# A four-layer graph network on one core: layers 1 to 3 as rounds of small steps in a fixed order

## The chip, the core and the metric

The kernel runs on one core of a Trainium2 chip. The metric is the device time of one execution in microseconds; the time of a kernel is the median of several executions.

The core's engines run beside each other and meet at semaphores. TensorE (PE in the profile; its weight loads are PEld) does matrix products and transposes and writes them to PSUM, eight banks of 128 x 512 fp32 here. VectorE (DVE) and ScalarE (ACT) do elementwise work and read PSUM. GpSimd (POOL) issues the indirect DMAs that gather rows by index. SyncE (SP) and ScalarE's queue issue the other transfers.

## The reference

`x` holds 4096 nodes of 256 features, `adj` is a symmetric 4096 x 4096 matrix of zeros and ones with ones on the diagonal; each entry off the diagonal is set with a chance of about 0.2%, so a node has some nine neighbours. Four graph attention layers follow each other, each on the layer-normed input and added to it:

```python
h = jnp.maximum(_layernorm(x, axis=-1), 0.0); x = x + _L0_gnn_ref(...)   # 8 heads, curvature bias
h = jnp.maximum(_layernorm(x, axis=-1), 0.0); x = x + _L1_gnn_ref(...)
h = jnp.maximum(_layernorm(x, axis=-1), 0.0); x = x + _L2_gnn_ref(...)
h = jnp.maximum(_layernorm(x, axis=-1), 0.0); x = x + _L3_gnn_ref(...)

# layer 1: one head
h = node_features @ W.T + b_W
e = (h @ a1)[:, None] + (h @ a2)[None, :] + b_a[0]
e = jnp.where(e > 0, e, 0.2 * e)
attention = jax.nn.softmax(jnp.where(adjacency_matrix > 0, e, NEG_INF), axis=1)
h_prime = attention @ h

# layer 2: e of both signs (e the leaky_relu of Wh1 + Wh2.T), then one product
h_prime = softmax(where(mask, e, NEG_INF)) @ inp
h_prime_negative = -softmax(where(mask, -e, NEG_INF)) @ inp
elu(concatenate([h_prime, h_prime_negative], axis=1) @ wtrans)

# layer 3: four heads of 64
h = x @ w.T + bias
score = leaky_relu(h @ h.T, 0.01)
coeff = softmax(where(adj > 0, score, 1.0)); relu(coeff @ h)
```

## The kernel before

**Lists instead of the matrix.** Layer 0 finds each node's neighbours in `adj` and keeps them as lists; layers 1 to 3 use the lists only. Nodes lie in NT = 32 tiles of P = 128. For each tile the edges are sorted into EC = 9 chunks of 128, one edge on each partition. An *indirect DMA* fetches for every edge of a chunk the neighbour's row from a table in DRAM (`table1`, `table2`, `table3`, one for each layer, written tile by tile during the layer before): `gather`, L909, on GpSimd, one instruction for each chunk. The rows land in `g`, a buffer of nine chunks and the tile's own rows; there are G = 6 such buffers. `st` is a 0/1 matrix that says which edge belongs to which node of the tile, `s` the same with edges on the other side; `sw` is `s` weighted with the edge's softmax weight.

**What a tile needs.** The sum over neighbours, "attend", is a chain of matrix products of `sw` with `g` (`summed`, L930; in layer 2 `attend2`, L1919), and the last column gives the softmax's denominator, whose reciprocal `inv` is taken on VectorE by the step that finishes the tile. In layers 1 and 3 the ninth chunk (LATE) isn't gathered: its rows come from the table's last eighth, held in SBUF as three bf16 parts (`late_rows`), and are picked by a product with a 0/1 matrix `to` (`expanded`, L1701, then a copy to `g` on ScalarE, L1705). So layers 1 and 3 gather 8 chunks for each tile and layer 2 gathers 9.

- Layer 1: `marked` and `go_to` build `st` and `to` from the lists; `before1` spreads the nodes' scores over the edges by products with `st` (`by_edge`) and keeps `s` for layers 2 and 3 in DRAM (`s_of`; `st` and `to` go to `rows_of`); `weigh1` makes scores, exponentials and `sw`; `attend1`; `finish1` divides, adds to `x` and normalizes; `rows2` makes `table2`'s row by VectorE and ScalarE; `give2` makes layer 2's own scores for each edge.
- Layer 2: `weigh2` makes `sw` with both signs (L1897 to L1906); `attend2` two chains, one for each half of the tile's nodes; `signed2` scales both by their reciprocals (L1929 to L1934); `turn_signed` transposes (L1941) and copies to `two_t` (ScalarE, L1945); `through_wt` multiplies by `wtrans` (L1954); `finish2`, `turn3` and `rows3` make `x`, its transpose `hT` and `table3`'s row.
- Layer 3: `before3` casts `s` on ScalarE; `weigh3` spreads the tile's own rows over the edges (27 products into the PSUM buffers `pv`, L2056), multiplies by `g` on VectorE (L2060), sums within heads (L2061), takes the exponential and weights `g` (L2074); `attend3`; `finish3`.

**Order.** Layers 1 to 3 are each one call of `run` (L1714). It takes a list of steps with lags: the step of tile t is issued in round t + lag, and within a round in the order of the list. `loads` (lag -3), `begin` (the first 7 chunks of gathers, lag 2 - G = -4) and `begin_late` (the rest, later for the first tiles, as the end of the table is written last) are ahead of the list. Layer 3's list, for example:

```python
[(0, weigh3), (1, attend3), (-1, before3), (2, finish3), (-1, expand3), (-2, own_parts)]
```

TensorE runs in the order of this program (`manual_schedule`). VectorE, ScalarE, GpSimd and the DMA queues get their order from the scheduler, which sees the dependencies and a few `issue_after` hints; each engine runs its own list strictly in order. Layer 0 is ordered by a planner that the change leaves alone.

Of the kernel before, what the change touches and what calls it, by code (L numbers as in the profile page):

```python
# [9 lines left out]
F32 = mybir.dt.float32  # L10
# [694 lines left out]
BEHIND = 3  # L705
ROW0, ROW1, ROW3 = C + H0 + CF, C + 2, C
# [7 lines left out]
def gnn_lists(  # L714
# [917 lines left out]
    with tc.tile_pool(name="work", bufs=2) as work, tc.tile_pool(name="kept", bufs=1) as kept:  # L1632
# [9 lines left out]
        mine1 = kept.tile([P, MINE, P + 3], BF16, name="mine1")  # L1642
        nc.gpsimd.tensor_copy(mine1[:, :, :P], ident_b[:, None, :].to_broadcast([P, MINE, P]))

        def by_edge(pool, t, st, own_t):

            my = mine1[:, t % MINE, :]
            nc.any.tensor_copy(my[:, P:], upper(own_t))
            s, parts = spread(pool.tile([P, 3, 512], F32, name="s_ps"), st, my, P + 3)
            a = work.tile([P, EC + 1], F32, name="a", bufs=3)  # L1650
            nc.vector.tensor_reduce(a[:, :EC].rearrange("p (b c) -> p b c", c=3), parts, AX.X, OP.add)
            return s, a
# [31 lines left out]
        def go_to(t, to):  # L1684

            pm = bank(ps_e, "pe")[:, :P]
            nc.tensor.matmul(
                pm, lhsT=col_late[:, t : t + 1].to_broadcast([P, P]), rhs=ident, start=True, stop=True
            )
            nc.vector.tensor_tensor(  # L1690
                to.rearrange("p (b e) -> p b e", b=LB), pm[:, None, :].to_broadcast([P, LB, P]),
                late_no[:, :, None].to_broadcast([P, LB, P]), op=OP.is_equal,
            )

        def expanded(t, of, width, pool, name):

            to = of.pop("to")
            ps = bank(pool, name)[:, :width]
            for b in range(LB):
                for i in range(3):  # L1700
                    nc.tensor.matmul(  # L1701
                        ps, lhsT=to[:, b * P : (b + 1) * P], rhs=late_rows[:, b, i, :width],
                        start=(b == 0 and i == 0), stop=(b == LB - 1 and i == 2),
                    )
            nc.scalar.copy(of["g"][:, LATE, :width], ps)  # L1705
# [8 lines left out]
        def run(table, width, x_of, steps, first=None, expand=False, rows=True):  # L1714


            of, late = [{} for _ in range(NT)], {}

            def loads(t):
                two = t // 2 * 2  # L1720
                if t == two:
                    of[t]["ss"] = work.tile([P, 2, EC * P], BF16, name="ss", bufs=3)
                    if not first:
                        nc.sync.dma_start(of[t]["ss"], s_of[t // 2])
                of[t]["pair"] = of[two]["ss"]
                of[t]["s"] = by_slot(of[t]["pair"][:, t - two, :])
                if rows:
                    if t == two:
                        of[t]["sts"] = work.tile([P, 2, (EC + LB) * P], BF16, name="st", bufs=4)
                        if not first:  # L1730
                            nc.sync.dma_start(of[t]["sts"], rows_of[t // 2])
                    both = of[two]["sts"][:, t - two, :]
                    of[t]["st"], of[t]["to"] = both[:, : EC * P], both[:, EC * P :]
                if first:
                    marked(first, t, of[t]["st"])
                    go_to(t, of[t]["to"])
                    if t > two:
                        store(rows_of[t // 2], of[two]["sts"])
# [6 lines left out]
            def begin(t):  # L1745
                with ExitStack() as queue:
                    if t - BEHIND in late:
                        queue.enter_context(tc.issue_after(late.pop(t - BEHIND).ins))
                    of[t]["g"] = gather_early(t, table, width, g_pool)

            def begin_late(t):
                last = gather_late(t, of[t]["g"], table, width, range(EARLY, LATE if expand else EC))
                if t < G - BEHIND:
                    late[t] = last

            def late_lag(t):

                return (-1, -2, -2, -3, -3)[t] if t < 5 else 2 - G

            steps = [(-3, loads), (2 - G, begin), (late_lag, begin_late)] + [  # L1760
# [444 lines left out]
```

## Time and profile before

| | |
|---|---|
| median of 11 runs | 2046.18 us (2035.33 to 2054.24) |
| profiled execution, its own time | 2041.4 us |
| its span | 2039.6 us, granted TensorE clock 0.814 |
| layer 0, 1, 2, 3 in its trace | 0 to 735, to 1150, to 1635, to 2039.6 us |
| busy in the span | PE 69%, PEld 53%, DVE 57%, ACT 34%, POOL 54% |
| gathers | 1088 (288, 256, 288, 256), mean 981 ns, 1067.3 us in all |

Times in views are microseconds from the start of the span, and means are in ns. A number in brackets after an instruction is the idle time of its engine before it, with what released it. A matmul's end is modelled, not recorded. "issue" is time in which an engine waited for nothing that the profile shows; "remote" and "another core or an unknown queue" stand for a release whose source the profile does not find.

### The profile page before, as it was taken

The page shows a single profiled execution, that of the slowest core. Times are in us where ns is not written, and L with a number is a line of the kernel's source. Part 1 is how long each engine was busy: PE and PEld are TensorE (multiplying, and loading weights), DVE is VectorE, ACT ScalarE, POOL GpSimd, SP SyncE. Part 2 cuts the span into 40 slices and gives each one's busy share as a digit, 9 for nine tenths or more (in the row PEclk, how much of TensorE's full clock was granted, in tenths as well). Part 3 has the DMA queues.
Part 4 walks back from the last instruction along what each step waited for, and adds up shares of the span by engine and source line. Part 5 has one row for each costly group of instructions (what it writes and reads, how often), then busy time and mean ns, then how long its engine had stood idle before and what let it go on. Part 6 is the DMA issues. An engine that isn't in the chain of part 4 may idle for free.

```text
span 2039.6 us, 24838 instructions
## 1 busy us (share of the span) xinstructions
PE 1398.7 (69%) x7536; PEld 1081.6 (53%) x7536; DVE 1159.6 (57%) x3174; ACT 686.6 (34%) x1798; POOL 1095.3 (54%) x1179
## 2 busy tenths in 40 slices
PE   5735545757576765767578347888889478888886
PEld 3413434535454544556457235666668356666665
DVE  5635645756674544555356224555556258877886
ACT  4545434635442233333233013333334221111111
POOL 2063354445556457667565566666661456656640
PEclk9855767867777867788788669888889689989998
DMA  8866666766434455666567545555553356656630
GB/s 271 290 223 199 196 191 207 237 198 208 130 103 123 131 155 157 199 191 200 158 201 245 169 110 164 157 171 166 164 161 114 110 166 206 208 180 207 194 110 23
DMA packets 169888, 356.67 MB, mean 175 GB/s; under 512 B 32272, under 2 KB 104208, under 8 KB 169744
## 3 DMA queue, kind: packets, MB, share of 16 engines
q0 software_dynamic: 52224, 145.30, 26.9%
q1 hardware_dynamic: 67970, 143.98, 21.5%
q10 hardware_dynamic: 49550, 65.71, 9.1%
q8 instruction: 62, 1.02, 0.2%
q14 instruction: 82, 0.67, 0.1%
HBM read 291.66 MB, written 63.21 MB: 174 GB/s over the span
## 4 chain that ended last, share of the span: by engine, by line
PE 39%; DVE 18%; another core or an unknown queue 18%; issue 11%; ACT 5%; DMA 2%; POOL 1%; ACTq 0%; DVEq 0%; POOLq 0%; SPq 0%
PE o L930 20%; PE o L1919 5%; PE pt L1954 3%; PE pv L2056 2%; PE pt L874 2%; DVE g L2074 2%; PE pv L1701 2%; PE pe L1701 1%; DVE s L2061 1%; DVE v L2060 1%; POOL g L909 1%; DMA g<-table,nbr 1%; DVE sw L1897 1%; DVE g L1537 1%
## 5 line engine op out<-in xcount | busy, mean ns | idle before, releaser
L909 POOL DMA_INDIRECT g<-table,nbr x1088 | 1067.3, 981 | 763.4 <-issue 319.1
L930 PE MATMUL o<-g,sw 128*128 128x257 f32 (+1 forms) x1216 | 320.9, 423 | 6.8 <-remote 3.2
L930 PEld LDWEIGHTS o<-g,sw 128*128 128x128 f32 x1216 | 257.0, 214 | 55.0 <-issue 4.0
L1919 PE MATMUL o<-g,sw 128*128 128x257 f32 x896 | 207.9, 390 | 12.1 <-issue 12.1
L1919 PEld LDWEIGHTS o<-g,sw 128*128 128x128 f32 x896 | 177.7, 198 | 40.8 <-issue 12.2
L930 PE MATMUL o<-g,s_f 128*128 128x264 f32 x576 | 167.8, 456 | 0.0
L930 PEld LDWEIGHTS o<-g,s_f 128*128 128x128 f32 x576 | 136.0, 236 | 33.0
L1954 PE MATMUL pt<-wt_s,two_t 128*128 128x256 f32 x256 | 91.2, 518 | 60.1 <-ACT two_t L1945 57.6
L1204 ACT ACTIVATE mask<-adj,minus_half 128x1024 bf16<-128x1024 int32 x112 | 125.1, 1143 | 19.6 <-PE kps L1226 5.2
L2056 PE MATMUL pv<-parts,st 128*128 128x256 bf16 x864 | 111.4, 278 | 26.4 <-issue 21.9
L865 PE MATMUL pt<-ident,r 128*128 128x128 f32 x192 | 45.2, 324 | 106.4 <-DVE r L845 33.1
L2060 DVE TENSOR_TENSOR v<-pv,g 128x512 f32<-128x512 f32 (+1 forms) x160 | 94.0, 630 | 42.0 <-remote 29.6
L2056 PEld LDWEIGHTS <-st 128*128 128x128 bf16 x864 | 84.7, 100 | 49.5 <-issue 38.8
L1954 PEld LDWEIGHTS pt<-wt_s,two_t 128*128 128x128 f32 x256 | 63.7, 259 | 83.1 <-ACT two_t L1945 67.2
L2065 ACT ACTIVATE pm<-s 128x40 f32<-128x40 f32 x32 | 6.7, 208 | 297.9 <-DVE s L2063 240.5
L1701 PEld LDWEIGHTS <-st 128*128 128x128 bf16 x768 | 74.8, 100 | 49.9 <-issue 35.6
L2074 DVE SCALAR_TENSOR_TENSOR g<-pm,g 128x2560 f32<-128x2560 f32 x32 | 90.3, 2823 | 7.1 <-issue 5.8
L865 PEld LDWEIGHTS pt<-ident,r 128*128 128x128 f32 x192 | 25.8, 161 | 126.8 <-issue 57.1
L1537 DVE TENSOR_TENSOR g<-g,pt 128x2560 f32<-128x2560 f32 x32 | 90.1, 2815 | 1.9 <-ACT pt L1534 1.3
L874 PE MATMUL pt<-wcat,hT 128*128 128x272 f32 (+1 forms) x256 | 75.8, 422 | 15.1 <-issue 9.7
L930 PE MATMUL o<-g,ident 128*128 128x264 f32 (+1 forms) x128 | 57.7, 541 | 39.6 <-DVE g L2074 20.1
L2061 DVE TENSOR_REDUCE s<-v 128x36 f32<-128x2304 f32 x32 | 81.7, 2553 | 1.1
(360 smaller groups left out, 2344.6 us busy)
## 6 DMA issues: line engine op xcount, KB each, us to landing
adj<-in_adj_l SPq DMA_DIRECT2D x128, 512.0 KB
ss<-s_of SPq DMA_DIRECT2D x32, 576.0 KB
g<-table,nbr POOLq DMA_INDIRECT x1088
rows_of<-st ACTq DMA_DIRECT2D x16, 832.0 KB
st<-rows_of SPq DMA_DIRECT2D x16, 832.0 KB
x<-x SPq DMA_DIRECT2D x24, 512.0 KB
s_of<-ss ACTq DMA_DIRECT2D x16, 576.0 KB
table<-row ACTq DMA_DIRECT2D x32, 258.0 KB
```

Source lines behind the costliest of these rows:

```text
L874: nc.tensor.matmul(pp, lhsT=hT[:, k, :], rhs=w[:, k, :], start=(k == 0), stop=(k == KC - 1))
L909: last = nc.gpsimd.indirect_dma_start(out=g[:, c, :width], out_offset=None, in_=table[: NE if c < EARLY else N, :], in_offset=bass.Indirec ...
L930: nc.tensor.matmul(o, lhsT=a, rhs=b, start=(i == 0), stop=(i == len(pairs) - 1))
L1204: nc.scalar.activation(m, a, AF.Sign, bias=minus_half, scale=1.0)
L1537: nc.vector.tensor_mul(gh, gh, w[:, :, :, None].to_broadcast([P, K, H0, D0]))
L1701: nc.tensor.matmul(ps, lhsT=to[:, b * P : (b + 1) * P], rhs=late_rows[:, b, i, :width], start=(b == 0 and i == 0), stop=(b == LB - 1 and i ...
L1919: nc.tensor.matmul(o, lhsT=sw[:, h, i].rearrange("p s r -> p (s r)"), rhs=g[:, c, : C + 1], start=(i == 0), stop=(i == HC + 1),)
L1954: nc.tensor.matmul(pp, lhsT=lhs[:, k, :], rhs=wt_s[:, k, :], start=(k == 0), stop=(k == 2 * KC - 1))
L2056: nc.tensor.matmul(pv[:, k, :], lhsT=st[:, (a + k) * P : (a + k + 1) * P], rhs=parts[:, i, :], start=(i == 0), stop=(i == 2),)
L2060: nc.vector.tensor_mul(v[:, a : a + n, :], pv[:, :n, :], g[:, a : a + n, :C])
L2061: nc.vector.tensor_reduce(s[:, :EC, :], heads(v, K3), AX.X, OP.add)
L2074: weighed3[t] = nc.vector.scalar_tensor_tensor(gh, w[:, :, :, None].to_broadcast([P, K, K3, D3]), -math.e, gh, op0=OP.add, op1=OP.mult,)
```

## The change

The steps of layers 1 to 3 are cut into smaller ones, most of them with work for one engine, and get new lags and a new order. A step that reads what TensorE wrote (`take1`, `go_to`, `take2`, `take_signed`, `take3`, `low2`, `row3`, `multiply3`, the `finish` steps) is now apart from the one that made it, and is issued at another place of the round or a round later. In rounds 0 to 31 of each layer, `in_order` adds an ordering dependency without a semaphore between each two successive instructions of VectorE and of ScalarE, so these two run in the order in which the program issues them.

```diff
+        def in_order(first):
+            traced = nc.cur_bb.bb.instructions
+            for engine in (nc.vector.engine, nc.scalar.engine):
+                mine = [i for i in traced[first:] if i.engine == engine]
+                for a, b in zip(mine, mine[1:]):
+                    tc.add_manual_dep(b, a.name, mybir.DependencyInfo(
+                        mybir.DependencyClass.NoSync, mybir.DependencyReason.DATA), reason="round")
...
-            def late_lag(t):
-                return (-1, -2, -2, -3, -3)[t] if t < 5 else 2 - G
-            steps = [(-3, loads), (2 - G, begin), (late_lag, begin_late)] + [
+            lead = last_use + 1 - G
+            def late_lag(t):
+                return first_use - 1 + t // 2 - t if t < 5 else lead
+            steps = [(-3, loads), (lead, begin), (late_lag, begin_late)] + [
...
             for r in sorted(rounds):
+                if r == 0:
+                    start = len(nc.cur_bb.bb.instructions)
+                if r == NT + 0:
+                    in_order(start)
...
-                    (3, give2), (0, weigh1), (2, finish1), (1, attend1), (-1, before1),
-                    (2, rows2), (-1, expand1),
-                first=only, expand=True,
+                    (-1, take1), (-1, score1), (0, attend1), (-3, go_to), (3, take2), (1, finish1),
+                    (2, store2), (-3, off1), (-1, weigh1), (-2, spread1), (-2, expand1), (-3, mark1), (-4, look_up),
+                    (2, give2), (1, rows2), (-3, keep_rows),
+                last_use=0, first_use=-1, rows=True,
...
-                    (0, weigh2), (1, signed2), (2, finish2), (0, attend2), (2, turn3), (1, turn_signed),
-                    (2, rows3), (1, through_wt),
-                rows=False,
+                    (-1, score2), (0, attend2(0)), (2, through_wt), (-1, weigh2), (1, signed2), (3, turn3),
+                    (3, take3), (0, attend2(1)), (4, row3), (2, low2), (1, turn_signed), (4, parts3), (2, finish2),
+                    (3, rows3), (1, take_signed),
+                last_use=0, first_use=-1, late=2, s=True,
...
-            name="l3_v", bufs=5, space=PSUM
+            name="l3_v", bufs=1, space=PSUM
...
+            def products3(t, of, first, last):
+                for i in range(first, last):      # pv0 to pv4, a bank each
+                    ...
             def expand3(t, of):
-                if t:
-                    expanded(t, of, C, ps_v, "pv")
+                pv = bank(ps_v, f"pv{GV - 1}").rearrange("p (k c) -> p k c", c=C)
+                of.setdefault("pv", {})[GV - 1] = pv
+                expand_to(pv[:, 1, :], of.pop("to"), C)
+            def spread3(t, of):
+                products3(t, of, 0, GV - 1)
+            def take3(t, of):
+                nc.scalar.copy(of["g"][:, LATE, :C], of["pv"][GV - 1][:, 1, :])
+            def last3_of(t, of):
+                products3(t, of, GV - 1, GV)
...
-                [(0, weigh3), (1, attend3), (-1, before3), (2, finish3), (-1, expand3), (-2, own_parts)],
-                expand=True,
+                    (-3, own_parts), (5, out3), (1, total3), (1, full3), (0, multiply3), (2, attend3),
+                    (0, score3), (0, exp3), (3, finish3), (4, add3), (-1, expand3), (-1, spread3),
+                    (-1, take3), (-1, last3_of), (0, weigh3),
+                last_use=2, first_use=0, s=True, rows=True,
```

`lead` makes the early gathers' lag -5 in layers 1 and 2 and -3 in layer 3, where attend moves from lag 1 to lag 2; the number of buffers stays 6. In layer 3 the five PSUM buffers `pv`, used in turn by `expand3` and the products, become `pv0` to `pv4` with one place each, and `expand3` writes the second half of `pv4`, whose first half `last3_of` fills. Some work changes engines: in layers 1 and 2 the copy of one column for each tile goes from ScalarE to VectorE; in layer 3 the self weight (VectorE, L2066) becomes a ScalarE activation, and `finish3`'s product with `inv` (VectorE) becomes four ScalarE activations (Relu with a scale), followed by an addition on VectorE in `add3`. Stores move with their steps: `table2` to `store2` (a round later than `finish1`), `xs[1]` to `rows2`, `out` to `out3`.

## The prediction

> **What bounds the kernel now.** I read the page's chain first, then POOL's groups by layer, the timeline around the longest gap, and a table of stretches. The chain by engine, from the page:
>
> ```profile
> PE 39%; DVE 18%; another core or an unknown queue 18%; issue 11%; ACT 5%; DMA 2%; POOL 1%; ACTq 0%; DVEq 0%; POOLq 0%; SPq 0%
> ```
>
> There is one core, so 18% "another core" (some 360 us when its pieces are added up, about 200 of it in layers 1 to 3) has no such cause. I looked for what those pieces have in common. The longest, as the timeline has it (start, duration, engine, instruction, idle time before and its releaser):
>
> ```profile
> 1176.16 0.60 PE L1941 MATMUL pt<-ident,two 128*128 128x128 f32 x4
> ...
> 1183.43 0.17 DVE L1929 RECIPROCAL inv<-o 128x1 f32<-128x1 f32 x1 [7.52 <-remote]
> 1197.82 0.95 POOL L909 DMA_INDIRECT g<-table,nbr  x1 [0.30 <-issue]
> 1203.05 0.32 SPq L923 DMA_DIRECT2D g<-table  x1
> 1203.06 0.17 DVE L1929 RECIPROCAL inv<-o 128x1 f32<-128x1 f32 x1 [19.14 <-remote]
> 1203.29 0.94 POOL L909 DMA_INDIRECT g<-table,nbr  x1 [4.53 <-remote]
> 1204.65 1.65 PE L1954 MATMUL pt<-wt_s,two_t 128*128 128x256 f32 x3 [27.89 <-ACT two_t L1945]
> ```
>
> TensorE had finished `attend2` by about 1176.3, yet VectorE took the product 7 and 27 us later. In between GpSimd gathered without a break from 1154.3 to 1198.8 (35 gathers); 4 us after its last one everybody who waited for TensorE went on at the same moment. The other long pieces (14.3 us at 770, 17.0 at 967, 15.2 at 1130, 15.7 at 1601) fall in the same way into unbroken runs of 24 to 28 gathers. So in this trace a product of TensorE is seen late while GpSimd gathers on; after a run of 8 or 9 gathers the lag is 2 to 4 us. The reason is not shown; the pattern is.
>
> GpSimd's gathers by layer (layers 1, 2, 3; busy us, mean ns, idle before and what ended it):
>
> ```profile
> L909 POOL DMA_INDIRECT g<-table,nbr x228 | 235.7, 1034 | 114.0 <-issue 62.0 <-PE o L930 21.1 <-remote 9.3
> ```
> ```profile
> L909 POOL DMA_INDIRECT g<-table,nbr x260 | 255.7, 983 | 140.8 <-issue 72.9 <-remote 21.8 <-PE pt L865 19.0
> ```
> ```profile
> L909 POOL DMA_INDIRECT g<-table,nbr x228 | 215.7, 946 | 147.4 <-issue 60.0 <-DMA table<-row 26.2 <-PE pv L2056 21.5
> ```
>
> At 0.30 us between gathers, a tile costs POOL 8 × 1.334 = 10.7, 9 × 1.283 = 11.5 and 8 × 1.246 = 10.0 us. The attends came every 12.0, 13.4 and 11.7 us. The rest of POOL's idle time is waiting for TensorE to free a buffer `g`: 114.0 − 228 × 0.30 = **45.6**; 140.8 − 260 × 0.30 − 12.5 (before the first gather, the table's write) = **50.3**; 147.4 − 68.4 − 26.2 = **52.8**; together 148.7 us.
>
> Is a compute engine the bound instead? The stretches (window; length, PE, PEld, DVE, ACT, POOL busy; PE clock, DMA share, GB/s):
>
> ```profile
> 743.50:1090.50 347.00, 240.57 (x1427) 190.17 (x1428) 180.96 (x590) 126.46 (x296) 235.74 (x228) 0.79 0.63 187
> 1090.00:1105.00 15.00, 15.00 (x123) 12.90 (x121) 11.43 (x41) 7.49 (x21) 0.00 (x0) 1.00 0.85 284
> 1154.00:1539.00 385.00, 291.74 (x1206) 237.88 (x1206) 185.45 (x521) 119.22 (x498) 255.71 (x260) 0.85 0.55 159
> 1540.00:1577.00 37.00, 36.67 (x165) 30.54 (x166) 25.44 (x71) 18.25 (x77) 0.00 (x0) 0.95 0.29 97
> 1638.50:1976.50 338.00, 275.57 (x1689) 218.49 (x1687) 259.49 (x327) 52.19 (x138) 215.69 (x228) 0.96 0.59 186
> 1977.00:2009.00 32.00, 29.28 (x197) 24.65 (x196) 30.80 (x42) 7.54 (x19) 0.00 (x0) 1.00 0.06 19
> ```
>
> No. Each layer has a stretch in which all gathers are done (POOL 0). There the same code runs a tile in 6.5 us (attends at 1091.39, 1097.89, 1104.58), 9.7 (1544.77, 1554.42, 1564.21) and 9.5 (1981.85, 1992.00, 2001.20, 2010.30). The engines can do a round in less than POOL needs; what they lack while POOL gathers is timely sight of TensorE's products.
>
> **The change, part by part.** The sum goes against the profiled execution's own time, 2041.4 us (span 2039.6); the median of the runs shown is 2046.2, 4.8 above it.
>
> *Layer 0* keeps its order up to its very end: 0 (its 162 us of such gaps stay).
>
> *Work added.* Two `[P,1]` copies a tile go from ScalarE to VectorE (0.16 to 0.19 us), layer 3's `y` product (0.424), the self weight (0.290) and the last step (0.418) become five ScalarE activations and one VectorE addition (0.42). VectorE's layer 3 round falls from about 9.8 to 9.1 us, ScalarE's rises from 2.3 to about 3.6. Both lie beside POOL's 10.0, so 0 as long as POOL sets the round; without that cover 0.7 × 32 = 22 us gained. PE gains two instructions in 21,500: 0.
>
> *Order and lags.* By before's durations a round needs at most 8.2 us on PE, 7.6 on VectorE, 4.8 on ScalarE (layer 1), 10 / 7.7 / 6.0 (layer 2), 9.8 / 9.1 / 3.6 (layer 3). In layers 1 and 3 most products are now taken a round (some 10 us) after they are made, in layer 2 half a round. What waits for what changes: `through_wt` no longer stands right behind `turn_signed` in PE's queue, where it waited for ScalarE's `two_t`, with `attend2` of the next tile queued behind it. The strict order is also a price: a VectorE instruction that waits for a late product now holds all that is listed behind it. That is covered while the lag is under the slack (2 to 4 us against 10, and about 3 in layer 2); it fails when POOL runs on for several tiles.
>
> *POOL's pauses.* POOL must pause when no buffer is free, and after a pause the products are seen. Its shortest steady pauses are 2.0 to 2.1 us, once a tile (layer 3: gathers resume at 1872.08, 1883.78, 1895.62, 1907.40). With a round of slack a pause every second tile does, which halves the sum: bounds 0 (one per tile stays) and 148.7 (none); I take half, **−74**.
>
> *Tails.* From the last gather to the last attend pass 36.7, 51 and 49.7 us, as up to six full buffers are worked off. With TensorE closer behind POOL there are fewer: 0 to −60; I take **−20**, one round less in each layer and a little off.
>
> *Drains.* Lags of 3 to 5 instead of 2 add up to two short rounds of steps behind the last attend, of which little is on the path: 0 to +15, I take **+5**.
>
> *DMAs.* Stores (`table2`, `xs`, `rows_of`, `s_of`) move with their steps to later places in ScalarE's queue. They are consumed layers later or, for the tables, behind late gathers that wait 12.5 and 26.2 us at the layer's start already: 0, ±10.
>
> Sum: −74 − 20 + 5 = −89, so 2041.4 − 89 = 1952 for the profiled execution, **1957** with the 4.8.
>
> [...] A gather took 946 ns in layer 3, where VectorE was busy 259.5 of 338 us, and 1034 in layer 1 at 181 of 347: a denser VectorE did not slow it, so the row gives 0. [...] The granted clock was 0.79, 0.85 and 0.96 in the three stretches with gathers, and 0.50 in the stall at 1130 to 1160. [...]
>
> **The rivals.** *All pauses go.* For it: the stretches above show engines fit for 6.5 to 9.8 us a tile. Then 2041.4 + 4.8 − 148.7 − 60 + 5 = 1842.
>
> *It doesn't do what it says.* If one pause per tile is what lets products be seen at all, POOL's round stays, and only the stalls at the layers' starts and a few of layer 2's gaps go: 2000 to 2045. For it: in layer 3 every pause ends just as VectorE is released (1895.38 and 1895.62).
>
> *Slower: layer 3's shared bank.* `pv` falls from five rotating buffers to five names of one each, and `expand3` shares `pv4` with the last products: `last3_of` waits until ScalarE's `take3` has copied `expand3`'s half. On PE attend takes 5.2 us and expand 1.5; the 24 products between them and `last3_of` last 2.8, and the copy 0.37: a slack of 2.4 us. A round is then 9.8 + (lag − 2.4), which passes before's 11.7 from a lag of **4.3 us** on. With 7 us, as seen at 1183.43, it is 14.4: +2.7 × 31 = 84. With nothing gained elsewhere 2041.4 + 4.8 + 84 + 5 = 2135; with half the pauses gone in layers 1 and 2, 2087. Against it: POOL then pauses longer, and pauses shorten the lag.
>
> **How the numbers follow.** The main case (1900 to 2000) gets 0.50, all pauses gone (1800 to 1900) 0.17, no effect (2000 to 2060) 0.15, the shared bank or a like wait behind the strict order (2060 to 2150) 0.18. The forecast is 1957. The range, 1865 to 2085, leaves out about 0.09 on either side. A difference under 0.3% (6 us, about what a measurement of this kernel can tell) needs 2040 to 2052: 0.05. Faster: 0.50 + 0.17 + 0.06 = 0.73; slower 0.22. Of the main case alone the range is 1900 to 2000.
>
> **What would show it.** Right: POOL's idle time beyond 0.30 us a gather falls from 148.7 to about 75, the attends come every 10.7 to 11.2 us in layers 1 and 3 and about 12.5 in layer 2; "another core" shrinks in layers 1 to 3 alone; `through_wt`'s waits for `two_t` (47.2 us after 1204) are gone. Wrong: PE waits for `take3`'s copy ahead of `last3_of`, or VectorE's and ScalarE's waits for "remote" grow with runs of 16 and more gathers; or POOL's pause stays at 2 us per tile. [...]

## The result and the profile after

The changed kernel takes **2060.12 us** (median of 13 runs, 2041.95 to 2073.84) against 2046.19 us before (50 runs): ratio 1.0078, 95% interval 1.0048 to 1.0108. So it is slower by 0.8%, some 16 us, where 1957 and a gain were forecast. A ratio leaves out executions in a slower state of the chip, so it can differ a little from the quotient of two medians.

The profiled execution has a span of 2069.1 us. Its chain by engine:

```profile
PE 29%; another core or an unknown queue 19%; DVE 18%; issue 14%; ACT 7%; POOL 4%; DMA 2%; ACTq 0%; DVEq 0%; POOLq 0%
```

TensorE's share of the chain fell (39% to 29%), but "another core" did not shrink, and "issue" grew. GpSimd's gathers in layers 1, 2 and 3 (windows 743.5 to 1090, 1155 to 1538, 1632 to 2006; busy us, mean ns, idle before):

```profile
L910 POOL DMA_INDIRECT g<-table,nbr x228 | 233.2, 1023 | 116.0 <-issue 72.4 <-ACT g L1840 10.6 <-ACT w L1856 10.1
```
```profile
L910 POOL DMA_INDIRECT g<-table,nbr x261 | 258.9, 992 | 125.0 <-issue 72.4 <-remote 23.0 <-PE o L1979 10.9
```
```profile
L910 POOL DMA_INDIRECT g<-table,nbr x229 | 217.3, 949 | 157.9 <-issue 98.1 <-ACT pm L2163 21.0 <-ACT pm L2162 19.9
```

Less 0.30 us a gather, 47.6 + 46.7 + 89.2 = 183.5 us are left, where the prediction hoped for about 75. These windows leave out the waits before the first gathers of layers 2 and 3. With them, GpSimd's idle time beyond 0.30 us a gather, from the first gather of layer 1 to the last of layer 3, is (us; "again" are the traces of the first experiment below):

| | before | after | before again | after again |
|---|---|---|---|---|
| within layer 1 | 57.3 | 59.5 | 63.5 | 54.8 |
| wait for layer 2's first gather | 15.4 | 30.5 | 14.6 | 29.2 |
| within layer 2 | 62.9 | 46.9 | 63.1 | 47.3 |
| wait for layer 3's first gather | 38.9 | 46.2 | 42.1 | 47.5 |
| within layer 3 | 79.2 | 102.6 | 84.1 | 104.9 |
| in all | 253.7 | 285.7 | 267.4 | 283.7 |

The 32.0 us more account for the 29.5 us by which the span grew. Layer 3 is the larger part; what layer 2 gains, it loses at its start. The two first gathers, before and after, with the idle time before them:

```profile
1105.40 0.94 POOL L909 DMA_INDIRECT g<-table,nbr  x1 [15.70 <-DVE s L1777]
1577.48 0.94 POOL L909 DMA_INDIRECT g<-table,nbr  x1 [39.17 <-DVE inv L1929]
```
```profile
1120.32 0.98 POOL L910 DMA_INDIRECT g<-table,nbr  x1 [30.82 <-DVE sw L1861]
1584.34 0.94 POOL L910 DMA_INDIRECT g<-table,nbr  x1 [46.50 <-PE o L1979]
```

The early chunks read the first seven eighths of the table, so these gathers need the rows of the 28th tile. In layer 1 that tile was divided at 1096.0 and its rows' store issued at 1100.3 before; after, at 1103.0 and 1113.0, as `store2` comes a round later. That the gather waited for this store is read from the code and the times; the releasers named in the lines don't show it.

The pauses did not go away; in layer 3 they became fewer and longer. Before, GpSimd mostly gathers 8 there and pauses 2.0 to 2.1 us. After, runs of 16 take turns with runs of 8; after a run of 16 it pauses 5.2 to 9.4 us, after a run of 8 some 2.2 to 2.5. The stretch from 1725 shows what happens in such a run (it began at 1725.28, and the last gather ended at 1744.98; other rows of the timeline are left out):

```profile
1725.28 0.94 POOL L910 DMA_INDIRECT g<-table,nbr  x1 [2.45 <-ACT g L2141]
...
1731.43 1.49 PE L1685 MATMUL pv<-late_rows,st 128*128 128x256 bf16 x12
1732.75 2.23 PE L2127 MATMUL pv<-parts,st 128*128 128x256 bf16 x19
1735.23 0.27 PE L2127 MATMUL pv<-parts,st 128*128 128x256 bf16 x1 [0.24 <-issue]
1736.67 0.27 PE L2127 MATMUL pv<-parts,st 128*128 128x256 bf16 x1 [1.17 <-issue]
1737.37 0.38 PE L2127 MATMUL pv<-parts,st 128*128 128x256 bf16 x2 [0.43 <-issue]
1738.75 0.27 PE L2127 MATMUL pv<-parts,st 128*128 128x256 bf16 x1 [1.00 <-issue]
1744.03 0.95 POOL L910 DMA_INDIRECT g<-table,nbr  x1 [0.30 <-issue]
1746.47 0.37 ACT L2141 COPY g<-pv 128x256 f32<-128x256 f32 x1 [13.80 <-remote]
1746.89 0.80 PE L2127 MATMUL pv<-parts,st 128*128 128x256 bf16 x3 [7.87 <-issue]
1747.93 2.81 DVE L2152 TENSOR_TENSOR v<-pv,g 128x512 f32<-128x512 f32 x5 [13.26 <-PE pv L2127]
1754.42 0.95 POOL L910 DMA_INDIRECT g<-table,nbr  x1 [9.44 <-ACT pm L2163]
```

`expand3` was done at 1732.9, but ScalarE's `take3` saw it at 1746.5, 1.5 us after the last gather: 13.5 us late. TensorE itself slowed from 1735 on, though the profile shows nothing that its products wait for; the last three, at 1746.89, follow `take3`, which frees their bank. In the seven runs of 16 gathers of layer 3 `take3` is 6.5 to 13.6 us late, otherwise between 0 and 3.4. The stretches in numbers (length, PE, PEld, DVE, ACT, POOL busy; clock, DMA share, GB/s):

```profile
1725.00:1735.00 10.00, 9.98 (x70) 8.53 (x68) 9.31 (x11) 2.89 (x10) 7.56 (x8) 1.00 0.68 229
1735.00:1747.00 12.00, 1.30 (x6) 0.51 (x6) 0.00 (x0) 0.41 (x2) 7.57 (x8) 0.70 0.37 110
1747.00:1754.00 7.00, 7.00 (x30) 5.71 (x29) 5.93 (x9) 1.69 (x5) 0.00 (x0) 0.79 0.76 234
```

In the first 10 us of the run TensorE got 138 products and weight loads done and was busy all the time; in the next 12 us it got 12. I counted its instructions from the start of each run of 15 or more gathers to the first product before which TensorE stood idle for over 0.35 us and the profile names "issue". From layer 2 on there are 17 such runs: the count is 122 to 136 in eleven, 154 to 174 in three, 95 in one, and two runs at the start of layer 3 show no such place (a few records are missing). In layer 1 it scatters from 20 to 180. There the products of an attend then start in steps of 0.70 us (at 1037.22, 1037.93, 1038.64, 1039.36, 1040.06) or twice that, instead of 0.22 to 0.43.

What that does to the engines that wait for TensorE shows in the waits of 1680 to 2040 that end with "remote" (sum, times, longest), before and after:

```profile
DVE v L2060 <- remote: 21.5, 24, 2.2
DVE inv L2086 <- remote: 13.1, 11, 1.4
ACT g L1705 <- remote: 5.9, 1, 5.9
```
```profile
DVE v L2152 <- remote: 87.4, 14, 13.6
ACT g L2141 <- remote: 60.9, 9, 13.8
```

For VectorE and ScalarE together they grew from 40.5 to 148.3 us.

The time between divisions tells what that does to a layer. From a layer's 5th tile to its 29th (layer 3: 25th), before and after: 11.7 and 11.9 us a tile in layer 1 (823.0 to 1103.5; 824.8 to 1110.8), 13.0 and 12.9 in layer 2 (1248.0 to 1560.9; 1252.5 to 1562.8), **12.0 and 13.1 in layer 3** (1714.5 to 1954.2; 1731.1 to 1993.4). The divisions of layer 3 no longer come evenly but as 1731.1, 1753.6, 1762.6, 1771.9, 1794.4, 1803.4, 1812.5, 1833.5: two or three rounds of 9 to 10 us, then one of 21 to 23.

### The profile page after: what moved, and what is told of

The parts are those of the page before. It is cut to its first block, busy times and chain, and to the rows that moved or that the text cites. A ratio compares the mean times of both kernels' runs of the same rounds, so it can differ in the third digit from the quotient of the medians.

```text
span 2069.1 us, 24939 instructions
## 1 busy us (share of the span) xinstructions
PE 1418.9 (69%) x7536; PEld 1085.1 (52%) x7536; DVE 1151.6 (56%) x3158; ACT 718.3 (35%) x1910; POOL 1094.2 (53%) x1179
## 4 chain that ended last, share of the span: by engine, by line
PE 29%; another core or an unknown queue 19%; DVE 18%; issue 14%; ACT 7%; POOL 4%; DMA 2%; ACTq 0%; DVEq 0%; POOLq 0%
PE o L931 12%; PE o L1979 5%; POOL g L910 4%; DVE v L2152 2%; DVE s L2157 2%; PE pt L875 2%; PE pt L2021 2%; PE pv L2127 2%; DMA g<-table,nbr 2%; DVE stats L843 1%; PE pe L1685 1%; DVE g L1538 1%; DVE sw L1957 1%; PE pt L1525 1%
## 5 line engine op out<-in xcount | busy, mean ns | idle before, releaser
L931 PE MATMUL o<-g,sw 128*128 128x257 f32 (+1 forms) x1216 | 347.8, 432 | 70.4 <-issue 48.7
L1979 PE MATMUL o<-g,sw 128*128 128x257 f32 x896 | 227.9, 400 | 63.2 <-issue 62.6
L2127 PEld LDWEIGHTS <-st 128*128 128x128 bf16 x864 | 85.2, 99 | 67.9 <-issue 56.8
L1685 PEld LDWEIGHTS <-st 128*128 128x128 bf16 x768 | 79.8, 106 | 67.3 <-issue 49.8
L866 PE MATMUL pt<-ident,r 128*128 128x128 f32 x128 | 33.3, 353 | 102.6 <-DVE r L846 29.9
L1957 DVE TENSOR_TENSOR sw<-ss,w 128x640 f32<-128x640 bf16 x64 | 50.0, 823 | 63.0 <-remote 27.1
L2021 PE MATMUL pt<-wt_s,two_t 128*128 128x256 f32 x256 | 65.5, 401 | 23.8 <-ACT two_t L2012 20.3
L837 ACT ACTIVATE rstd<-mv,eps 128x1 f32<-128x1 f32 (+1 forms) x104 | 30.5, 293 | 140.4 <-DVE mv L844 47.6
L866 PEld LDWEIGHTS pt<-ident,r 128*128 128x128 f32 x128 | 17.7, 175 | 117.3 <-issue 60.2
```

Of the source, the lines that this page charges most:

```text
L931: nc.tensor.matmul(o, lhsT=a, rhs=b, start=(i == 0), stop=(i == len(pairs) - 1))
L1685: nc.tensor.matmul(ps, lhsT=to[:, b * P : (b + 1) * P], rhs=late_rows[:, b, i, :width], start=(b == 0 and i == 0), stop=(b == LB - 1 and i ...
L1979: nc.tensor.matmul(o, lhsT=sw[:, h, i].rearrange("p s r -> p (s r)"), rhs=g[:, c, : C + 1], start=(i == 0), stop=(i == HC + 1),)
L2021: nc.tensor.matmul(pp, lhsT=lhs[:, k, :], rhs=wt_s[:, k, :], start=(k == 0), stop=(k == 2 * KC - 1))
L2127: nc.tensor.matmul(pv[:, k, :], lhsT=st[:, c * P : (c + 1) * P], rhs=parts[:, j, :], start=(j == 0), stop=(j == 2),)
```

## The experiments

The theory, called A or A2 in the expectations: in a run of gathers what TensorE finishes is seen late, the later the more of its instructions have gone before in the run, and after some 130 of them it almost stops; the change makes the runs of layer 3 longer. The rivals: the strict order (B), the shared bank (A1), TensorE's time (C), layer 3's order as such (D).

The chips differed in a way that was not expected. On some the kernel before has a median of 2046 to 2069 us, as in the result; on others, where a part of the experiments ran, it is 1612 to 1614. Each experiment is therefore compared with the kernel before on its own chip, and those on the second kind stand together at the end.

**The changed kernel and the kernel before again, beside each other.**

> The changed kernel again, beside the kernel before on one chip. On the chip of the first experiments the kernel before took 1611.6 us instead of 2046, gathers ran without a pause through whole layers, and TensorE's products were seen within 0.01 us. Theory A (the change moves where TensorE stands still in runs of gathers, and in layer 3 it makes the runs longer): where the kernel before takes about 2046, the changed one takes 2050 to 2070; where it takes about 1612, TensorE never stands still, GpSimd is the bound, and the changed kernel is within 30 us of before, slower by the longer drains (+5 to +25). Rival B (the strict order is the price by itself): slower by 14 us or more on either chip.

> The kernel before, unchanged, for its trace on the same chip as the others of this set. Theory A: where it takes about 2046 us, the longest idle times of VectorE fall into runs of 20 and more gathers, and TensorE slows after about 128 of its instructions in such a run; where it takes about 1612, GpSimd pauses nowhere in layers 1 to 3 and the chain is GpSimd's. Rival: the difference between chips is spread over all engines (slower instructions), which would show in the mean durations.

2060.37 against 2045.53 us: ratio 1.0077 (1.0036 to 1.0118); the kernel before took 2050 in its profile. From the 5th to the 25th tile layer 3 took 244.5 us before and 263.0 after, as in the first pair of traces (239.7 and 262.3). The result holds.

**Layer 3 as before.** Layers 1 and 2 of the changed kernel, then layer 3's old steps with the old `run` (parts of the edit):

```diff
-            name="l3_v", bufs=1, space=PSUM
+            name="l3_v", bufs=5, space=PSUM
...
-                    (-3, own_parts), (5, out3), (1, total3), (1, full3), (0, multiply3), (2, attend3),
-                    (0, score3), (0, exp3), (3, finish3), (4, add3), (-1, expand3), (-1, spread3),
-                    (-1, take3), (-1, last3_of), (0, weigh3),
...
+                [(0, weigh3), (1, attend3), (-1, before3), (2, finish3), (-1, expand3), (-2, own_parts)],
```

> Layers 1 and 2 as in the changed kernel, layer 3 as before, once more, as the first such run fell on a chip on which the kernel before took 1612 us. Theory A, where the kernel before takes about 2046: by the traces of both kernels layer 3 costs 45 us more after the change, layer 2 15 less, layer 1 nothing: 2015 to 2030 us. Rival B (the strict order costs in each layer): 2050. Where it takes about 1612: 1636 again.

2041.18 us; ratio 0.9996 (0.9955 to 1.0036). With the old layer 3 the loss is gone. But the gain of 15 to 30 us that I read from the traces did not come either; layers 1 and 2, with the waits at the layers' starts (28.2 and 45.9 us here), come to nothing that this run can tell, less than half a per cent.

**The shared bank.** The last three products of a tile move ahead of `expand3`, so that no copy by ScalarE lies between two writes of TensorE to `pv4` (the order of the steps; the steps' own small changes are left out):

```diff
-                    (0, score3), (0, exp3), (3, finish3), (4, add3), (-1, expand3), (-1, spread3),
-                    (-1, take3), (-1, last3_of), (0, weigh3),
+                    (0, score3), (0, exp3), (3, finish3), (4, add3), (-1, last3_of), (-1, expand3), (-1, spread3),
+                    (-1, take3), (0, weigh3),
```

> The changed kernel with the last three products of a tile ahead of expand3 in the shared bank pv4, so that TensorE never waits for take3 of its own round; nothing else changes. Theory A1 (the shared bank alone makes layer 3 slower), where the kernel before takes about 2046: TensorE's idle 7 to 8 us in every third round go, -45, about 2015. Theory A2 (TensorE's products are seen late in long runs of gathers, whatever it waits for, because its signals queue up behind some 130 instructions): the wait moves to VectorE's multiply3 and to attend3, less than 15 us are gained. Where it takes 1612: no difference beyond 5 us.

2059.69 us; ratio 1.0064 (1.002 to 1.0108): nothing is gained that could be told from the changed kernel. Its timeline shows the waits where theory A2 puts them, with ScalarE's and VectorE's sight of the products as late as before:

```profile
1745.11 0.37 ACT L2140 COPY g<-pv 128x256 f32<-128x256 f32 x1 [13.54 <-remote]
1745.18 2.81 DVE L2150 TENSOR_TENSOR v<-pv,g 128x512 f32<-128x512 f32 x5 [11.60 <-remote]
```

**Without the strict order.**

```diff
-                if r == NT + 0:
-                    in_order(start)
```

> The changed kernel without in_order, once more. Where the kernel before takes about 2046: rival B (a late product holds all that is listed behind it) -10 us or more against the changed kernel's 2060; theory A within 10 us. Where it takes 1612: 1622 again.

2051.83 us; ratio 1.0042 (0.9991 to 1.0092). It overlaps both kernels: the time alone leaves room for a cost of the strict order of nothing or of about 1%. The trace says more. Layer 3 still takes 13.1 us a tile from its 5th to its 25th (1699.3 to 1960.7), so the strict order is not what makes it slow. But the waits for the first gathers of layers 2 and 3 are 22.8 and 38.8 us, where the changed kernel has 30.8 and 46.5 (29.5 and 47.8 again): if the order costs anything, it is there, some 16 us in these single traces.

**Without GpSimd's gathers.** In layers 1 to 3:

```diff
         for c in chunks:
+            if width != ROW0:
+                end = NE if c < EARLY else N
+                last = nc.sync.dma_start(g[:, c, :width], table[end - P : end, :])
+                continue
             last = nc.gpsimd.indirect_dma_start(
```

> The changed kernel, whose layers 1 to 3 read fixed rows by plain transfers of SyncE's queue in place of GpSimd's indirect gathers (same sizes and buffers; which neighbour a row belongs to is left out). Theory A (GpSimd's gathers are what makes TensorE's products late), where the kernel before takes about 2046: no product is seen late in layers 1 to 3, rounds of 8.2, 10 and 9.8 us, layers 1 to 3 together about 1000 us instead of 1320, total 1720 to 1780. Rival (it is the transfers' traffic, or TensorE by itself): the jumps stay, over 1950. Where it takes 1612, both give 1600 to 1640.

1651.46 us in one run. Windows in the three layers:

```profile
742.00:1000.00 258.00, 217.56 (x1543) 186.37 (x1541) 207.26 (x691) 119.84 (x263) 0.00 (x0) 0.95 0.80 258
1030.00:1312.00 282.00, 281.64 (x1391) 245.54 (x1390) 198.57 (x585) 138.06 (x576) 0.00 (x0) 1.00 0.71 224
1369.00:1634.00 265.00, 264.38 (x1752) 228.89 (x1751) 247.98 (x288) 93.62 (x296) 0.00 (x0) 1.00 0.66 212
```

The DMA engines move more than before (212 to 258 GB/s, where the stretches with gathers of the kernel before had 159 to 187), and TensorE does not pause in layers 2 and 3 (busy 281.64 of 282.00 and 264.38 of 265.00 us). So it is not the traffic and not TensorE by itself; GpSimd's gathers are needed for the lateness (whether because they are indirect or because GpSimd issues them, this run does not tell). The rounds are 8.3, 9.1 and 8.6 us (first to last division over 31), where I had put down 8.2, 10 and 9.8; the shorter rounds of layers 2 and 3 are part of why the time lies under 1720 to 1780.

**More and fewer instructions on TensorE.** Two edits, the first in the kernel before, the second in the changed one (there `expand_to`, not shown, is cut from 12 products to 4 as well):

```diff
+                for _ in range(32):
+                    nc.tensor.matmul(whole[:, 300:303], lhsT=ident_b, rhs=ident_b[:, :3], start=True, stop=True)
...
-                        for j in range(3):
-                            nc.tensor.matmul(
-                                pv[:, k, :], lhsT=st[:, c * P : (c + 1) * P], rhs=parts[:, j, :],
-                                start=(j == 0), stop=(j == 2),
-                            )
+                        nc.tensor.matmul(
+                            pv[:, k, :], lhsT=st[:, c * P : (c + 1) * P], rhs=parts[:, 0, :],
+                            start=True, stop=True,
+                        )
```

> The kernel before with 32 products of 128x3 bf16 (64 instructions of TensorE, 0.8 us of its time) behind each attend of layer 3. Theory A (in a run of gathers TensorE lives on some 128 instructions): where the kernel before takes about 2046, each of layer 3's rounds, at 116 instructions, then needs 180, stands still within 8 gathers, and waits for a longer pause: +1.5 to +3 us a round, +50 to +100 in all. Rival C (what counts is TensorE's time, or the time since the run began): +0.8 us a round at most, 0 to +26 in all. Where the kernel before takes 1612, both say 0 to +26.

> The changed kernel, whose layer 3 multiplies with the first of three bf16 parts only (9 products instead of 27, 4 instead of 12 in expand3): the lower bits of the scores and of the late rows are left out. TensorE's instructions of a round fall from 122 to 70, its time by 2.8 us. Theory A: where the kernel before takes about 2046, a run of 16 gathers no longer exhausts TensorE, the jumps of 22 us between divisions go, and layer 3 comes to 10.5 us a tile instead of 12.9: -60 to -80 us against the changed kernel. Rival A1 (it is the shared bank alone): last3_of still waits for take3, -10 to -30. Where the kernel before takes 1612, GpSimd is the bound and both say 0 to -10.

32 small products: 2101.42 us in one run, +56. From the 5th to the 25th tile a round takes 14.3 us (1717.2 to 2004.2) instead of 12.2 on the same chip, but at the end, with all gathers done, 9.8 instead of 9.4. So the same 64 instructions cost 0.4 us without gathers and 2.1 with them. Fewer products: 2019.42 us in one run, 41 under the changed kernel; 11.8 us a tile instead of 13.1. That lies between the two expectations. GpSimd still gathers in runs of 16, but pauses only 2.9 to 3.8 us after them, and VectorE's and ScalarE's waits for "remote" in 1680 to 2040 fall from 148.3 to 47.0 us. Both go the way of theory A2. They don't fully tell instructions from time, though, as the products taken away are also 2.8 us of work (an estimate: 26 a round, and layer 3's products of 128x256 follow each other every 0.109 us in both traces).

**Shorter runs.** The test that decides. Layer 3 of the changed kernel with six GpSimd fills behind each tile's gathers (columns that nobody reads):

```diff
                 last = gather_late(t, of[t]["g"], table, width, range(EARLY, EARLY + late))
+                if width == ROW3:
+                    for _ in range(6):
+                        nc.gpsimd.memset(of[t]["g"][:, :, C + K3 :], 0.0)
```

> As e13, which fell on a chip where the kernel before takes 1613 us. Theory A2, where the kernel before takes about 2046: gathers in eights with some 2 us between, layer 3 every 12.0 us instead of 13.0, although GpSimd has 2 us a tile more to do: -20 to -35 against the changed kernel's 2060. Rival D (layer 3's new order is slow by itself): 0 to +30. Rival D2 (what blocks is a busy GpSimd, not its gathers): +60 or more. Where it takes 1613: 1681 again.

2062.11 us where the kernel before takes 2068.76: ratio **0.9962** (0.9929 to 0.9996), against 1.0077 (1.0036 to 1.0118) for the changed kernel without the fills, which was measured on another chip of this kind. GpSimd from 1700 to 1980 (busy, mean, idle before):

```profile
L910 POOL DMA_INDIRECT g<-table,nbr x186 | 176.4, 949 | 72.2 <-issue 51.6 <-ACT g L2144 10.2 <-PE pv L2130 5.0
L1748 POOL MEMSET g<- 128x100 f32 x138 | 25.6, 186 | 6.6
```

The gathers come in eights with 2.0 to 2.7 us between, and layer 3 takes 12.1 us a tile as forecast (5th tile 1735.9, 25th 1978.3), in rounds of 9 to 16 us instead of 9 to 23. The waits for "remote" in 1680 to 2040 are 30.3 us on VectorE and none on ScalarE. Work was added to GpSimd, whose gathers set the pace, and by the two ratios the kernel became 1.1% faster. Here fills on GpSimd do no harm (rival D2), nor does layer 3's new order as such (D); gathers without a break do. On this chip this version is a little faster than the kernel before.

**The chips on which the kernel before takes 1612 to 1614 us.** There a trace of layer 3 has no pause in GpSimd at all: 208 gathers with 0.30 us between them, from 1320 to 1580 in the first experiment below:

```profile
L910 POOL DMA_INDIRECT g<-table,nbr x208 | 197.3, 949 | 63.4 <-issue 58.2 <-DVE v L2234 2.1 <-PE pv L2230 1.5
```

No engine waits for "remote" in this window, "another core" is missing from the chain, and GpSimd is the bound. Gathers take as long as elsewhere (949 ns); the difference is in when TensorE's products are seen. Layer 0, which the change leaves alone, has part in it too: layer 1's first gather starts at 526 to 531 us here and at 685 to 700 elsewhere. The changed kernel itself did not run on such a chip.

> Layers 1 and 2 as in the changed kernel, layer 3 as in the kernel before. Theory A (the loss sits in layer 3, where TensorE waits behind the bank that expand3 shares, and where runs of two tiles of gathers starve it): by the traces layer 3 from its first to its last division costs 45 us more after the change than before, layer 2 some 15 us less, layer 1 nothing; so about 2060 - 45 = 2015 to 2030 us, faster than the kernel before by 15 to 30. Rival B (the strict order costs as much in each layer): about 2050 us, between the two kernels.

1635.88 us, ratio 1.0157 (1.0133 to 1.0181).

> Layer 2 alone as in the changed kernel, layers 1 and 3 as before. Theory A: 2046 - 15 = about 2031 us, and the same as with layer 1 changed too. Rival B: over 2046.

In this kernel layers 1 and 3 have the old steps and the old `run`, layer 2 the new ones. 1629.29 us, ratio 1.0113 (1.0087 to 1.0138).

> The changed kernel without in_order: VectorE and ScalarE are ordered by the scheduler again, steps and lags stay. Rival B (a late product holds all that stands behind it in the fixed order): faster than the changed kernel by 10 us or more. Theory A (TensorE itself stands still, so nobody has anything to do): within 10 us of the changed kernel, or slower, if the scheduler puts steps late.

1622.51 us, ratio 1.0075 (1.0051 to 1.01). Where TensorE never stands still, the new steps cost 0.7 to 1.6% in these three forms, 24, 18 and 11 us. The traces show where. Within each layer GpSimd's pauses come to 1.2 to 3.4 us only. The waits for the first gathers of layers 2 and 3 are 6.5 and 21.0 us in the first form, 0.3 and 19.3 in the second, 0.3 and 15.1 in the third; where layers 1 and 2 are those of the kernel before (the runs with 8 large products below), 0.3 and at most 0.5. So nearly all of the cost is that the next layer's gathers start later.

> The changed kernel, with expand3's product in a PSUM bank of its own (the exponentials w move from PSUM to SBUF for it), so that last3_of no longer waits for take3. Theory A1 (the shared bank is what costs layer 3 its time): TensorE's idle time before the last three products goes, rounds near 11 us, 2060 - 45 = about 2015. Rival A2 (TensorE stands still in a long run of gathers whatever it waits for; after some 128 of its instructions in such a run it gets only one in 0.7 us): the stall moves to the next products, layer 3 gains less than 15 us, 2045 to 2060.

The edit moves `expand3` to the bank `pm` and `w` to SBUF. 1689.15 us, ratio 1.0487 (1.0462 to 1.0512). It could not decide about the bank here, but it showed something else: layer 3's gathers take 1207 ns instead of 949 (1320 to 1580, and below it the same window of the run without the strict order):

```profile
L910 POOL DMA_INDIRECT g<-table,nbr x174 | 210.0, 1207 | 53.0 <-issue 46.9 <-ACT y L2193 1.2 <-DMA g<-table 1.2
L2169 DVE SCALAR_TENSOR_TENSOR g<-w,g 128x2560 f32<-128x2560 f32 x24 | 67.9, 2828 | 8.8 <-ACT w L2161 8.8
```
```profile
L910 POOL DMA_INDIRECT g<-table,nbr x209 | 198.3, 949 | 63.7 <-issue 58.2 <-PE pv L2125 1.2 <-ACT pm L2161 0.9
```

> The changed kernel with six short GpSimd fills (columns of g that nobody reads, about 0.3 us each) behind each tile's eight gathers in layer 3, so that gathers run in eights with some 2 us between, as layer 3 of the kernel before has them. Theory A2 (TensorE's signals queue up in a run of gathers and pass when it ends; runs of 16 exhaust some 130 instructions): the slow stretches of TensorE inside runs go, layer 3 comes every 12.0 us instead of 13.0, although GpSimd has 2 us a tile more to do: -20 to -35 against the changed kernel. Rival D (layer 3's new order is slow by itself): GpSimd's extra work is added, 0 to +30. Rival D2 (what blocks is a busy GpSimd, not its gathers): no gap is left for the signals, +60 or more.

> Layer 3 of the changed kernel with the first of three bf16 parts only, once more, for an interval: the single time was 2019 us, 41 under the changed kernel. Theory A2: 2015 to 2030, ratio to before 0.985 to 0.993. If it was chance: 2045 to 2060.

With the fills 1680.66, ratio 1.0426 (1.0407 to 1.0445), 67 us over the kernel before. GpSimd's pauses within layer 3 come to 51 us in its trace, against 1.2 to 3.4 in the other runs on such chips; most of the rest are the waits at the layers' starts (6.3 and 20.9). Fewer products: 1633.09, ratio 1.0135 (1.011 to 1.0159), between the three forms above: no gain shows where TensorE is in time.

> The kernel before with 8 products of 128x248 bf16 (16 instructions of TensorE, 0.86 us of its time) behind each attend of layer 3: as much time as the 32 small products, a quarter of the instructions. Theory A2 (instructions count): a quarter of their +2.2 us a round in the stretch with gathers, some +0.6, 10 to 25 us in all. Rival C (TensorE's time counts): the same +2.2 us a round, about +56.

> As e15, which fell on a chip where the kernel before takes 1613 us (there +26 us). Where the kernel before takes 2046 to 2069: theory A2 (the number of TensorE's instructions in a run of gathers counts): a quarter of the +2.2 us a round that 32 small products cost, and TensorE's own 0.86 us at most: +10 to +28 us in all. Rival C (TensorE's time counts, which is the same as that of the 32 small products): about +56.

The 8 large products took the place of the 32 small ones in the kernel before (`whole[:, 262:510]`, `rhs=late_rows[:, 0, 0, :248]`). 1639.12 and 1634.7 us, ratio of the latter 1.014 (1.0113 to 1.0168): +22 to +26, or 0.7 to 0.8 us for each of the 32 tiles, about what the products take (an estimate: 8 at the 0.109 us of the 128x256 ones make 0.87). Both fell on chips without the stall, so the control for the small products is missing where it was wanted.

> The changed kernel, whose layers 1 to 3 read fixed rows by plain (not indirect) transfers from GpSimd's queue, same sizes and buffers; which neighbour a row belongs to is left out. It tells whether the indirect gather matters or any transfer that GpSimd issues. If any: products are late as now, 1950 to 2060 us. If the indirect gather alone: as with SyncE's transfers, 1640 to 1720.

1471.63 us: without the indirect gathers the engines' own rounds of 8.2, 9.3 and 9.1 us show (5th to 25th tile in layers 1, 2 and 3: 605.1 to 768.5, 884.7 to 1071.4, 1226.2 to 1407.7). Whether plain transfers from GpSimd's queue make products late, this chip could not tell. But it gives a comparison of the chips: without gathers, from the first division of layer 1 to the last of layer 3, this run takes 882 us (573.6 to 1455.6), and the run with SyncE's transfers on a chip of the other kind 892 (742.2 to 1634.4).

## Why the prediction was wrong, point by point

- **What bounds the kernel.** Right: the lateness of TensorE's products in runs of gathers is what costs the time, and the engines need less than GpSimd. The run with SyncE's transfers (1651 us) and the chips without the lateness (1612) both show it.
- **Pauses, −74.** This is the step that failed. "With a round of slack a pause every second tile does" came true in part, as runs of 16 and of 8 gathers take turns, but not "which halves the sum": within the layers the pauses went from 199.4 to 209.0 us, with the waits for the first gathers from 253.7 to 285.7. I took the lag as 2 to 4 us, as seen after 8 gathers, and a round's slack of 10 us as cover. In runs of 16 gathers `take3` sees its product 6.5 to 13.6 us late, where its own slack had been put at 2.4, and before `multiply3` VectorE stands idle 11.3 to 13.6 us in seven of the eight long runs, more than the slack of a round; a pause after 16 gathers then lasts 5.2 to 9.4 us, more than two pauses of 2.0 to 2.1. That the lag comes from the length of the run is shown by the fills: with runs of 8 layer 3 is back at 12.1 us a tile. The prediction itself said that the cover "fails when POOL runs on for several tiles", and the sum rests on runs of two tiles. The condition was written down and not priced.
- **DMAs, 0 ± 10, and drains, +5.** The stores of the tables were put at 0, because the late gathers wait for them anyway. The early gathers wait too: those before the first gathers of layers 2 and 3 grew from 54.3 to 76.7 us. In layer 2 most of it is a shift, as the wait of 12.5 us before its late gathers is gone; within layer 2 the pauses fell by 16.0. On the chips without the lateness these waits are nearly all that the new steps cost.
- **Layer 3.** Forecast 10.7 to 11.2 us a tile, measured 13.1. Layer 2 (12.5 forecast, 12.9 measured) and layer 1 (11.9 measured) hardly moved.
- **Tails, −20.** From the last gather to the last division 35.7, 46.6 and 48.3 us are left of 56.0, 62.0 and 49.8. That is more than forecast, 37 us in layers 1 to 3, but the next layer's 5th tile is not earlier for it (1252.5 where it was 1248.0, 1731.1 where it was 1714.5). Its gathers start later, as said, and layer 2's start now holds a run of 54 gathers (1120.3 to 1188.5), with the first division at 1198.7 instead of 1167.3.
- **Rivals.** The slower side had 0.22, and its mechanism was named as the shared bank. In the trace it looks right: TensorE stands idle 7.9 us until `take3` is done, one of the signs of being wrong that the prediction named; the other, longer waits for "remote" in runs of 16, came too. Without the wait for the bank nothing is gained (1.0064). A wait that can be seen is not a cause when another as long stands behind it. "One pause per tile is what lets products be seen" was the rival nearest to what the runs show.
- **VectorE and the gathers.** The prediction read from its rows that a denser VectorE does not slow a gather (946 ns beside 259.5 of 338 us, 1034 beside 181 of 347); layer 3's gathers stayed at 949 ns, as the row had it. The run with `w` in SBUF shows a case in which the product beside a gather does slow it. With `w` in PSUM (the run without the strict order) a gather that overlaps `weigh3`'s big product takes 945 ns, with both operands in SBUF 1964 on average and up to 3566, beside 946 for those that don't overlap. Why is not shown.
- **Small readings.** The prediction put the granted clock of the stall from 1130 to 1160 at 0.50; the trace has 0.53 there and 0.50 from 1140 on. Its "two instructions in 21,500" for TensorE stand in no view: both traces have 7536 products and as many weight loads. Neither bears on the sum.

**What stays open.** Why gathers hold up TensorE, and why on some chips only. Of the instruction fetches of 16 KiB none starts in the stretch from 1735 to 1747 (the nearest are at 1722.9 and 1755.2). Whether the number of TensorE's instructions or their time counts is not settled; that 32 small products cost 2.1 us beside gathers and 0.4 without speaks for the number. And the changed kernel with and without fills was not measured on one chip.

## What to carry to other kernels

A slack that is read from a regular stretch holds for the length of run in that stretch only (here 2 to 4 us after 8 gathers, 6.5 to 13.6 in runs of 16): ask first whether the change lengthens the run, and take the lag from the longest run in the trace. When two engines get in each other's way, a short forced pause in the one that sets the pace can be faster than none (here 0.9962 with the fills against 1.0077 without), and an experiment that adds work there is a quick way to see it. Count the waits between stages too: a loss can move to where no window looks (here from 54.3 to 76.7 us). And compare on one chip: the kernel before differs by 430 us between two kinds of chip.

## What the hardware showed that was not expected

- In runs of GpSimd gathers, on the chips with 2046 to 2069 us, TensorE's products were seen up to 27 us late (made by 1176.3, taken at 1203.1 in the kernel before). In eleven of 17 long runs of the changed kernel, from layer 2 on, TensorE first stood idle after 122 to 136 instructions; in the slow stretches from 1037 and from 1735 its products mostly started 0.70 us or about twice that apart. What in layers 1 to 3 of the kernel before still waited for "remote" at the end of a long run went on 0.8 to 4.4 us after its last gather.
- The same kernel takes 2046 to 2069 us on some chips and 1612 to 1614 on others, with gathers of 949 ns in layer 3 on both.
- With `w`, one operand of `weigh3`'s big VectorE product, in SBUF instead of PSUM, the gathers beside that product took 1964 ns instead of 945, and all gathers from 1320 to 1580 took 1207 on average instead of 949 (that run against the one without the strict order, on one chip).
